# Router of a Flamingo block: ranks from bfloat16 marks added up on TensorE, scores from x itself, only selected rows normalized

## The chip, the cores and the metric

The kernel runs on one core of a Trainium2 chip. The metric is the device time in microseconds of one execution. The engines work side by side, each in its own order: TensorE (PE in the profile, its weight loads PEld), VectorE (DVE), ScalarE (ACT), GpSimd (POOL) and SyncE (SP), which issues most of the transfers.

## The reference, cut to what matters

`x` is 2 batches of 2048 rows of 512 floats. Four stages update it; the change lies between the first and the second.

```python
x = x + tanh(g_xattn[0]) * L0_xattn(layernorm(x), ctx)       # stage 1: cross attention, 16 heads
x = x + tanh(g_ffn[0])   * L0_ffn(layernorm(x), ...)         # stage 2: only 256 rows of a batch
x = x + tanh(g_xattn[1]) * L1_xattn(layernorm(x), ctx)       # stage 3
x = x + tanh(g_ffn[1])   * L1_ffn(layernorm(x), ...)         # stage 4

def L0_ffn(x, w_router, ...):           # x is already the layernorm of the stream
    scores = x @ w_router
    _, idx = top_k(scores, 256)         # in falling order; equal scores by index
    x_sel = x[idx]
    h = rmsnorm(x_sel, g1)              # then attention with a causal mask over the 256, and a gated FFN
    ...
    return x.at[idx].set(x_proc)        # all other rows come back as they are
```

So stage 2 needs, for each batch, the rank of every row's score among 2048, the 256 rows with the highest scores in order of rank, and for all rows `x + tanh(g)*layernorm(x)`.

## The kernel before, in words

The rows lie in 32 tiles of 128 rows (`x[0]` to `x[31]`, fp32, all in SBUF during stage 1), four tiles to a block of 512 rows, four blocks to a batch: eight blocks, n = 0 to 7, with `b, blk = divmod(n, 4)`.

`cross_attention` (L213) runs over units: 16 per block, one per head. In each unit it makes the scores on PE (`sc`, L271), the negated row maxima on DVE (`nmx`, L116), the exponentials on ACT (`A`, L119), their reciprocal sums on DVE (`rden`, L127), the scaling on POOL (`A`, L128), and two units later the transposes on PE (`tp`, L289) with their copy on DVE (`AT`, L290). Every fourth unit the values follow (`po`, L297, copied by ACT, L305), and after a block's sixteenth the output projection (`pp`, L315), which DVE adds to `x` (L324). The front of the next block (row statistics, `xn` by L101, transposes `ptr`, queries `pq` by L248) lies in between.

At the end of each unit `beside(u)` is called. It takes two steps of the generators in `pending`. After the last `x` of block n (L325) `router(n, tiles)` is put there. Its steps before the change:

- statistics of the block's four tiles of `x`, `rstd` (`rsqrt`, L82: one instruction on DVE, a power on POOL), and `keep_mul`, `keep_add` (L450 to L454);
- for each tile: the normalized rows `xn` (L101), stored to `xn_d` (L460); their dot product with `w_router` (`ws`, L462, its accumulator is the `score`); then ACT makes `x*keep_mul + keep_add` in place (L466), stored to `x_d` (L473), from which stage 3 reads;
- `spread` (L497): the block's 512 scores are laid along the free axis of all partitions: four transposes of a broadcast column (`pb`, L78) and a copy by ACT (`sb`, L504). `sb` holds the scores of the batch so far;
- `count` (L490): one DVE instruction compares a stretch of `sb` with a tile's own scores, one per partition, and sums over the stretch into a column of `cnt`. Every earlier tile is compared with the new 512 scores, and each new tile with all scores so far; for a tile with itself, `jd` (L514) does it twice, masked with `before` and `after`, so that equal scores go by index;
- after a batch's last block `add_up` sums `cnt` to `rank` (L520), and `gather` makes one-hot rows of the ranks (`oh`, L537), multiplies them with row numbers on PE (`pi`, L541), and fetches the 256 rows from `xn_d` into `xs` by two indirect transfers (L557).

PSUM during stage 1: `mm` has two buffers, `sc` four, and the tag `o` two, which `tp`, `po`, `pb` and `pi` share.

The order on each engine is fixed ahead of time by a planner. It goes by the order in the program, but takes a later instruction first where the earlier one is not ready by its reckoning: in the trace the statistics of the first two tiles of block 7 stand at 521.9 us, ahead of the `x` of its third tile at 527.9 us, though the program has them after.

After block 7 there is no further unit. `while pending: beside(None)` then runs the last router to its end. Stage 2 begins with loads of `wqkv` (L654) and with `rms_block(xs, ...)` (L626): squares on ACT (L631), `rsqrt`, `hn` on DVE (L634), transposes (`ptr`, L110) and `hT` (L639), from which PE makes the values `pv` (L674).

Of the kernel before, what the change touches and what calls it, by code (L numbers as in the profile page):

```python
# [10 lines left out]
F32 = mybir.dt.float32  # L11
# [32 lines left out]
def flamingo_kernel(ctx: ExitStack, tc: tile.TileContext, a: dict, out: bass.AP):  # L44
# [329 lines left out]
    score = selp.tile([P, NT], F32, name="score")  # L374
    xs = [selp.tile([P, D], F32, name=f"xs{i}") for i in range(4)]

    xn_d = [dramp.tile([S, D], F32, name=f"xn_d{b}") for b in range(B)]
    x_d = [dramp.tile([S, D], F32, name=f"x_d{b}") for b in range(B)]

    idx = selp.tile([P, 4], mybir.dt.uint32, name="idx")  # L380
# [11 lines left out]
    with ExitStack() as st:  # L392
# [11 lines left out]
            allow_small_or_imprecise_dtypes=True,  # L404
        )

        before = rp.tile([P, P], F32, name="before")
        nc.gpsimd.memset(before, 1.0)
        nc.gpsimd.affine_select(
            out=before,  # L410
            in_=before,
            compare_op=ALU.is_gt,
            fill=0.0,
            base=0,
            pattern=[[-1, P]],
            channel_multiplier=1,
        )
        after = rp.tile([P, P], F32, name="after")
        nc.gpsimd.memset(after, 1.0)
        nc.gpsimd.affine_select(  # L420
# [21 lines left out]
        def router(n, tiles):  # L442

            b, blk = divmod(n, NBLK)
            t0 = n * TB
            mv, rstd = ln_stats([x[t0 + i] for i in range(TB)], "ln2")

            keep_mul = rp.tile([P, TB], F32, name="keep_mul", tag="keep_mul", bufs=2)
            keep_add = rp.tile([P, TB], F32, name="keep_add", tag="keep_add", bufs=2)
            nc.vector.tensor_scalar(keep_mul, rstd, gf[0], None, ALU.mult)  # L450
            nc.vector.scalar_tensor_tensor(
                keep_add, mv[:, :, 0], -1.0, keep_mul, ALU.mult, ALU.mult
            )
            nc.vector.tensor_scalar(keep_mul, keep_mul, 1.0, None, ALU.add)  # L454
            yield
            for i in range(TB):
                t = t0 + i
                xn = act.tile([P, D], F32, name="xn2", tag="xn2", bufs=2)
                normalize(xn, x[t], mv, rstd, i)
                nc.sync.dma_start(out=xn_d[b][ts(t - b * TPB, P), :], in_=xn)  # L460
                ws = act.tile([P, D], F32, name="ws2", tag="ws2", bufs=1)
                nc.vector.scalar_tensor_tensor(  # L462
                    ws, xn, 1.0, w_router, ALU.mult, ALU.mult,
                    accum_out=score[:, t : t + 1],
                )
                nc.scalar.activation(  # L466
                    x[t],
                    x[t],
                    AF.Identity,
                    scale=keep_mul[:, i : i + 1],  # L470
                    bias=keep_add[:, i : i + 1],
                )
                nc.sync.dma_start(out=x_d[b][ts(t - b * TPB, P), :], in_=x[t])  # L473
                yield
            for work in ranks(b, blk):
                work()
                yield

# [1 line left out]

        def ranks(b, blk):

            done, end = blk * BLK, (blk + 1) * BLK

            def own(t):
                return score[:, b * TPB + t : b * TPB + t + 1]

            def count(t, lo, hi, op, k):  # L490
                junk = rp.tile([P, S], BF16, name="junk", tag="junk", bufs=2)
                nc.vector.tensor_scalar(
                    junk[:, lo:hi], sb[b][:, lo:hi], own(t), None, op, ALU.add,
                    accum_out=cnt[b][:, t, k : k + 1],
                )

            def spread():  # L497
                if blk == 0:
                    sb[b] = rp.tile([P, S], F32, name="sb", tag="sb")
                    cnt[b] = rp.tile([P, TPB, 7], F32, name="cnt", tag="cnt")  # L500
                    nc.gpsimd.memset(cnt[b], 0.0)
                pb = ps_o.tile([P, BLK], F32, name="pb", tag="o")
                bcast_rows(pb, score[:, ds(b * TPB + blk * TB, TB)], ident)
                nc.scalar.copy(sb[b][:, done:end], pb)  # L504

            def new(t):
                lo, hi = t * P, (t + 1) * P
                if lo > 0:
                    count(t, 0, lo, ALU.is_ge, 0)
                if hi < end:  # L510
                    count(t, hi, end, ALU.is_gt, 1)
                jd = rp.tile([P, 2, P], BF16, name="jd", tag="jd", bufs=2)
                for k, (op, m) in enumerate(((ALU.is_ge, before), (ALU.is_gt, after))):
                    nc.vector.scalar_tensor_tensor(  # L514
                        jd[:, k, :], sb[b][:, lo:hi], own(t), m, op, ALU.mult,
                        accum_out=cnt[b][:, t, 2 + k : 3 + k],
                    )

            def add_up():
                nc.vector.tensor_reduce(rank[:, ts(b, TPB)], cnt[b], AX.X, ALU.add)  # L520
                gather(b)

            work = [spread]
            work += [
                lambda t=t: count(t, done, end, ALU.is_gt, 3 + blk - t // TB)
                for t in range(blk * TB)
            ]
            work += [lambda t=t: new(t) for t in range(blk * TB, (blk + 1) * TB)]
            return work + [add_up] if blk == NBLK - 1 else work

        def gather(b):

# [2 lines left out]
            for t in range(TPB):  # L535
# [4 lines left out]
                for r in range(2):  # L540
                    nc.tensor.matmul(  # L541
                        pi[r],
                        oh[:, ts(r, P)],
                        place[:, t, :],
                        start=(t == 0),
                        stop=(t == TPB - 1),
                    )
            pl = rp.tile([P, 2, 2], F32, name="pl", tag="pl")
            for r in range(2):
                nc.vector.tensor_copy(pl[:, r, :], pi[r])  # L550
# [5 lines left out]
            for r in range(2):  # L556
                nc.gpsimd.indirect_dma_start(  # L557
                    out=xs[b * 2 + r],
                    out_offset=None,
                    in_=xn_d[b][:, :],  # L560
                    in_offset=bass.IndirectOffsetOnAxis(
                        ap=idx[:, b * 2 + r : b * 2 + r + 1], axis=0
                    ),
# [33 lines left out]
    with ExitStack() as st:  # L597
# [25 lines left out]
        def wide(name):  # L623
            return keepp.tile([P, DC, BLK], F32, name=name, tag="wide", bufs=2)

        def rms_block(tiles, gcol, dst, pool, ps, tag, name):  # L626

            ss = pool.tile([P, 4], F32, name=name + "_ss", tag="rms_ss")
            hn = [pool.tile([P, D], F32, name="hn", tag="hn", bufs=4) for _ in tiles]
            for i, t in enumerate(tiles):  # L630
                nc.scalar.activation(hn[i], t, AF.Square, accum_out=ss[:, i : i + 1])  # L631
            r = rsqrt(4, ss, 1.0 / D, 1e-6, small, name + "_r")
            for i, t in enumerate(tiles):
                nc.vector.tensor_scalar(hn[i], t, r[:, i : i + 1], None, ALU.mult)  # L634
            transpose_block(
                ps,
                tag,
# [6 lines left out]
        with ExitStack() as sa:  # L644
# [19 lines left out]
            for k in (0, 2):  # L664
                make_causal_mask(nc, mask[:, k, :], NEG)

            hT = wide("hT")
            rms_block(xs, g1, hT, act, ps_tp, "tp", "rms1")

            v2 = act.tile([P, 4, D], F32, name="v2")  # L670
            for i in range(4):
# [687 lines left out]
```

## Time and profile before

| What | Value |
|---|---|
| Median of 3 runs | 1853.16 us (1852.38 to 1861.52) |
| Profiled execution: time, span | 1854.16 us, 1852.5 us |
| Busy, of the span | PE 90%, DVE 71%, ACT 57%, POOL 28% |
| Stage 1 with all routers | 0 to about 565 us |
| Counting: instructions of L492, of L514 | 102, 64 |
| One-hots, products with row numbers | 32, 64 |
| Stage 2 after the gather | 573 to about 827 us |

The span is what the profiler records between the first and the last instruction; the execution's own time has 1.7 us around it. Busy time of an engine counts only where it computes; PE's records overlap, so that a busy PE is not a PE at its limit. In the timeline a row has its start, its length, the engine, the line of the program, output and inputs by name, shapes, and in brackets how long the engine stood idle before it and for whom.

### The profile page before, as it was taken

The page shows a single profiled execution, that of the slowest core. Times are in us where ns is not written, and L with a number is a line of the kernel's source. Part 1 is how long each engine was busy: PE and PEld are TensorE (multiplying, and loading weights), DVE is VectorE, ACT ScalarE, POOL GpSimd, SP SyncE. Part 2 cuts the span into 40 slices and gives each one's busy share as a digit, 9 for nine tenths or more (in the row PEclk, how much of TensorE's full clock was granted, in tenths as well). Part 3 has the DMA queues.
Part 4 walks back from the last instruction along what each step waited for, and adds up shares of the span by engine and source line. Part 5 has one row for each costly group of instructions (what it writes and reads, how often), then busy time and mean ns, then how long its engine had stood idle before and what let it go on. Part 6 is the DMA issues. An engine that isn't in the chain of part 4 may idle for free.

```text
span 1852.5 us, 24500 instructions
## 1 busy us (share of the span) xinstructions
PE 1660.6 (90%) x7706; PEld 832.8 (45%) x7706; DVE 1311.2 (71%) x2769; ACT 1050.8 (57%) x3065; POOL 527.4 (28%) x666
## 2 busy tenths in 40 slices
PE   6989988888836989989999999999999999898969
PEld 3544544444413444445544454444444454443423
DVE  5777897887783642224537779889888888876966
ACT  2745544354501535304537778878787787754556
POOL 4534434342300320032214333322423243220200
PEclk9999999899967889999999999999999999998989
DMA  7011011011144009330011233334133133155465
GB/s 287 1 46 47 1 47 46 12 46 47 46 139 156 1 9 314 112 91 23 26 35 55 97 114 105 128 120 154 52 135 127 77 109 123 74 203 205 150 229 191
DMA packets 98456, 184.36 MB, mean 100 GB/s; under 512 B 11327, under 2 KB 30527, under 8 KB 94614
## 3 DMA queue, kind: packets, MB, share of 16 engines
q1 hardware_dynamic: 97430, 180.70, 28.1%
q0 software_dynamic: 896, 2.10, 0.6%
q8 instruction: 61, 1.00, 0.2%
q14 instruction: 69, 0.57, 0.1%
HBM read 108.31 MB, written 74.45 MB: 99 GB/s over the span
## 4 chain that ended last, share of the span: by engine, by line
PE 34%; DVE 14%; DMA 6%; ACT 5%; issue 2%; POOL 2%; SPq 1%; POOLq 0%; DVEq 0%; ACTq 0%
PE pp L315 8%; PE pq L248 7%; DVE h L1018 3%; PE ph L1002 3%; PE sc L271 2%; PE po L297 2%; PE pu L875 2%; PE pw L875 2%; PE acc L861 2%; PE tp L289 2%; PE po L1231 1%; DMA hf<-h_d 1%; DMA x<-h_d 1%; DVE u L1012 1%; DMA hq<-hq_d 1%
## 5 line engine op out<-in xcount | busy, mean ns | idle before, releaser
L119 ACT ACTIVATE A<-sc,nmx 128x128 f32<-128x128 f32 x1024 | 362.9, 377 | 171.7 <-DVE nmx L116 149.8
L128 POOL TENSOR_TENSOR A<-A,rden 128x512 f32<-128x512 f32 x256 | 274.4, 1073 | 479.9 <-DVE rden L127 373.1
L315 PE MATMUL pp<-L_wo,OT 128*128 128x512 f32 x768 | 365.9, 610 | 12.7 <-DVE x L324 4.7
L248 PE MATMUL pq<-xnT,L_wq 128*128 128x512 f32 x768 | 358.0, 612 | 0.2 <-ACT xnT L237 0.2
L119 ACT ACTIVATION_READ_ACCUMULATOR A<-sc,nmx 128x1 f32 x1024 | 221.4, 216 | 0.0
L248 PEld LDWEIGHTS pq<-xnT,L_wq 128*128 128x128 f32 x768 | 145.7, 197 | 159.6 <-issue 151.7
L116 DVE TENSOR_REDUCE nmx<-sc 128x4 f32<-128x512 f32 x256 | 169.2, 678 | 66.6 <-PE sc L271 66.5
L290 DVE COPY AT<-tp 128x512 f32<-128x512 f32 x256 | 172.8, 677 | 55.5 <-PE tp L289 55.1
L315 PEld LDWEIGHTS pp<-L_wo,OT 128*128 128x128 f32 x768 | 139.0, 195 | 159.6 <-issue 134.9
L1018 DVE SCALAR_TENSOR_TENSOR h<-u,cw,h 128x512 f32<-128x512 f32 x256 | 191.4, 782 | 5.6 <-ACT h L1014 5.1
L289 PE MATMUL tp<-ident,A 128*128 128x128 f32 x1024 | 164.3, 282 | 28.7 <-POOL A L128 26.6
L271 PE MATMUL sc<-L_kT,qT 32*128 32x128 f32 (+1 forms) x2048 | 164.0, 291 | 8.1 <-ACT A L119 5.1
L271 PEld LDWEIGHTS sc<-L_kT,qT 32*128 32x128 f32 (+1 forms) x2048 | 130.8, 189 | 87.2 <-issue 59.3
L289 PEld LDWEIGHTS tp<-ident,A 128*128 128x128 f32 x1024 | 119.3, 143 | 103.9 <-issue 48.0
L1231 PE MATMUL po<-w2q,hq 128*128 128x512 bf16 x512 | 121.2, 392 | 18.2 <-DVE hq L1213 8.5
L1014 ACT ACTIVATE h<-u,cb,cw 128x512 f32<-128x512 f32 x128 | 99.2, 809 | 64.7 <-DVE u L1012 60.1
L1002 PE MATMUL ph<-xiT,w1q 128*128 128x512 bf16 x512 | 125.1, 381 | 2.6 <-DVE u L1012 2.3
L297 PE MATMUL po<-AT,L_v 128*32 128x512 f32 (+1 forms) x512 | 115.9, 623 | 7.9 <-DVE AT L290 7.5
L305 ACT COPY OT<-po 128x512 f32<-128x512 f32 x96 | 55.7, 588 | 101.4 <-PE po L297 100.9
L1012 DVE TENSOR_TENSOR u<-ph,inv_b 128x512 f32<-128x512 f32 x128 | 85.1, 683 | 31.8 <-PE ph L1002 26.9
L1011 POOL COPY u<-carry 128x2 f32<-128x2 f32 x128 | 49.2, 386 | 192.0 <-DVE h L1018 159.6
L311 POOL TENSOR_TENSOR x<-x,L_bo 128x512 f32<-128x512 f32 x64 | 87.3, 1382 | 33.8 <-DMA x<-x_d 14.3
(216 smaller groups left out, 2203.3 us busy)
## 6 DMA issues: line engine op xcount, KB each, us to landing
h_d<-h SPq DMA_DIRECT2D x28, 1024.0 KB, 3.9
x_d<-x SPq DMA_DIRECT2D x64, 256.0 KB, 2.5
hf<-h_d SPq DMA_DIRECT2D x64, 256.0 KB, 3.3
x<-x_d SPq DMA_DIRECT2D x61, 256.0 KB, 4.5
x<-h_d SPq DMA_DIRECT2D x48, 256.0 KB, 5.7
x<-in_x SPq DMA_DIRECT2D x32, 256.0 KB, 5.4
xn_d<-xn SPq DMA_DIRECT2D x32, 256.0 KB
xf<-x_d SPq DMA_DIRECT2D x32, 256.0 KB, 3.8
```

Source lines behind the costliest of these rows:

```text
L116: nc.vector.tensor_reduce(nmx, sc, AX.X, ALU.max, negate=True)
L119: nc.scalar.activation(out_tile[:, h, :], sc[:, h, :], AF.Exp, bias=nmx[:, h : h + 1], accum_out=den[:, h : h + 1],)
L128: nc.gpsimd.tensor_tensor(out_tile, out_tile, rden.unsqueeze(2).to_broadcast([P, n, width]), ALU.mult,)
L248: nc.tensor.matmul(pq, W.wq[:, d, ts(e, P)], xnT[:, d, :], start=(d == 0), stop=(d == DC - 1),)
L271: nc.tensor.matmul(sc[h][:, t, :], qT[e % cpg][r, ts(t, P)], W.kT[r, b, e, :], start=True, stop=True,)
L289: nc.tensor.transpose(tp[:, t, :], A[:, t, :], ident)
L290: nc.vector.tensor_copy(AT, tp.rearrange("p t n -> p (t n)"))
L297: nc.tensor.matmul(po[h * dh : (h + 1) * dh, :], W.v[:, b, ts(hd, dh)], AT[c * hpc + h], start=True, stop=True,)
L315: nc.tensor.matmul(pp, OT[e][:, ts(i, P)], W.wo[:, e, :], start=(e == 0), stop=(e == nE - 1),)
L1002: nc.tensor.matmul(ph, w1q[:, d, ts(c, P)], xiT[g][:, d, :], start=(d == 0), stop=(d == DC - 1),)
L1018: nc.vector.scalar_tensor_tensor(z, u[:, ds(k, BLK)], cw[:, c, k : k + 1], z, ALU.mult, ALU.add)
L1231: nc.tensor.matmul(po, rows(c), w2q[:, c, :], start=(c == 0), stop=(c == HC - 1))
```

## The change

- Each comparison writes its marks, 0 or 1 in bfloat16, and does not sum them. A product on PE with a column block of 32 ones (`onesb`) adds up the marks over the partitions, so that one PSUM row holds, for 512 rows of x, how many of the tile's 128 rows go before each. Earlier tiles against the new scores go to partitions `32*blk` on (`old`); new tiles against all scores so far go to partitions `32*c` for block c (`new`). The sums stay in `cnt` (128 x 512), and after the last block four products with `pick`, a matrix that selects partitions 0, 32, 64 and 96, turn them into `rank`. A tile with itself needs one masked comparison (`tie`) instead of two.
- `marks` has four buffers, `tie` four; `junk` and `jd` had two each.
- The score is worked out from `x`: `rstd*(x.w) - mean*rstd*sum(w)`. `x` itself is stored to `x1_d`, and the row for stage 3 goes to a tile of its own, `xo`.
- The gather fetches from `x1_d`; the 512 selected rows get their layer norm after it, and the mean square of the normalized row is taken from its variance, so that the squares on ACT fall away for this call of `rms_block`.
- There are more and smaller steps: two for each tile of the scores, one for two marks, and `gather` pauses after every fourth one-hot.

```diff
+        w_sum = rp.tile([P, 1], F32, name="w_sum")
+        nc.vector.tensor_reduce(w_sum, w_router, AX.X, ALU.add)
+        onesb = rp.tile([P, 32], BF16, name="onesb")
...
 # router
-            mv, rstd = ln_stats([x[t0 + i] for i in range(TB)], "ln2")
...
             for i in range(TB):
-                xn = act.tile([P, D], F32, name="xn2", tag="xn2", bufs=2)
-                normalize(xn, x[t], mv, rstd, i)
-                nc.sync.dma_start(out=xn_d[b][ts(t - b * TPB, P), :], in_=xn)
+                t = x[t0 + i]
+                nc.vector.bn_stats(st[:, i, :], t)
+                nc.vector.bn_aggr(mv[:, i, :], st[:, i, :])
+                yield
                 ws = act.tile([P, D], F32, name="ws2", tag="ws2", bufs=1)
                 nc.vector.scalar_tensor_tensor(
-                    ws, xn, 1.0, w_router, ALU.mult, ALU.mult,
-                    accum_out=score[:, t : t + 1],
+                    ws, t, 1.0, w_router, ALU.mult, ALU.mult, accum_out=dot[:, i : i + 1]
                 )
+                nc.sync.dma_start(
+                    out=x1_d[b][ts(t0 + i - b * TPB, P), :], in_=t
+                )
+                yield
+            rstd = rsqrt(TB, mv[:, :, 1], 1.0, 1e-5, small, "ln2_rstd")
...
+            nc.vector.scalar_tensor_tensor(shift, mv[:, :, 0], -1.0, rstd, ALU.mult, ALU.mult)
+            nc.vector.tensor_tensor(dot, dot, rstd, ALU.mult)
+            nc.vector.scalar_tensor_tensor(
+                score[:, ds(t0, TB)], shift, w_sum, dot, ALU.mult, ALU.add
+            )
...
+            for i in range(TB):
+                yield
+                xo = act.tile([P, D], F32, name="xo", tag="xo", bufs=2)
                 nc.scalar.activation(
-                    x[t],
-                    x[t],
+                    xo,
+                    x[t0 + i],
...
 # ranks
+            def goes_before(to, t, c0, c1, op):
+                nc.vector.tensor_scalar(to, sb[b][:, c0:c1], own(t), None, op)
+            def counted(psum, c, to, m, **kw):
+                nc.tensor.matmul(psum[32 * c : 32 * c + 32, to], onesb, m, **kw)
...
+            for j in range(blk):
+                m = marks()
+                for i in range(TB):
+                    goes_before(m[:, ts(i, BLK)], j * TB + i, lo, end, ALU.is_le)
+                    old.append(m[:, ts(i, BLK)])
+                    if i % 2:
+                        yield
...
+                po = ps_o.tile([P, BLK], F32, name="old", tag="o")
+                for i, m in enumerate(old):
+                    counted(po, blk, slice(0, BLK), m, start=(i == 0), stop=(i == len(old) - 1))
+                nc.vector.tensor_copy(cnt[b][rows, :], po[rows, :])
+                yield
...
+                goes_before(m[:, 0:mid], t, 0, mid, ALU.is_lt)
+                if mid < end:
+                    goes_before(m[:, mid:end], t, mid, end, ALU.is_le)
+                tie = rp.tile([P, P], BF16, name="tie", tag="tie", bufs=TB)
+                nc.vector.scalar_tensor_tensor(
+                    tie, sb[b][:, ts(t, P)], own(t), after, ALU.is_equal, ALU.mult
+                )
...
+            pn = ps_o.tile([P, BLK], F32, name="new", tag="o")
+            for i, m in enumerate(new):
+                for c in range(blk + 1):
+                    counted(pn, c, slice(0, BLK), m[:, ts(c, BLK)], start=(i == 0), ...)
+            for i, m in enumerate(ties):
+                counted(pn, blk, ts(i, P), m, start=False, stop=(i == TB - 1))
+                nc.vector.tensor_tensor(cnt[b][rows, :], pn[rows, :], cnt[b][rows, :], ALU.add)
...
+                pr = ps_o.tile([P, TB, NBLK], F32, name="pr", tag="o")
+                for q in range(TB):
+                    nc.tensor.matmul(
+                        pr[:, q, :], cnt[b][:, ts(q, P)], pick, start=True, stop=True
+                    )
...
 # gather
+                if t % 4 == 3:
+                    yield
-                    in_=xn_d[b][:, :],
+                    in_=x1_d[b][:, :],
...
 # start of stage 2
+            for b in range(B):
+                rows = xs[2 * b : 2 * b + 2]
+                mv, rstd = ln_stats(rows, f"lns{b}")
+                for i, t in enumerate(rows):
+                    normalize(t, t, mv, rstd, i)
+                ms = row.tile([P, 2], F32, name="ms", tag="ms")
+                nc.vector.tensor_tensor(ms, mv[:, :, 1], rstd, ALU.mult)
+                nc.vector.tensor_tensor(ms, ms, rstd, ALU.mult)
+                rs = rsqrt(2, ms, 1.0, 1e-6, row, "rms1_r")
...
-            rms_block(xs, g1, hT, act, ps_tp, "tp", "rms1")
+            rms_block(xs, g1, hT, act, ps_tp, "tp", "rms1", r)
```

## The prediction

> **What bounds the kernel now.** I read the page first, then the busy time of each engine in stretches that follow the router, the groups of VectorE (DVE), the waits, and the timeline of the end of stage 1. The page's chain of waits reaches back only to 686 us, so stage 1 is read from stretches. One stretch runs from a router's first store of `xn` to the next router's; columns are length, then busy us and count of PE, PEld, DVE, ACT, POOL, then TensorE clock, DMA share, GB/s.
>
> ```profile
> 116.90:174.10 57.20, 51.70 (x308) 27.42 (x308) 46.77 (x123) 30.88 (x141) 24.87 (x23) 1.00 0.10 38
> 174.10:235.60 61.50, 55.62 (x308) 29.84 (x308) 50.09 (x133) 31.18 (x141) 24.93 (x23) 0.94 0.10 35
> 235.60:300.70 65.10, 56.11 (x308) 29.76 (x308) 55.32 (x141) 31.16 (x141) 24.99 (x23) 0.95 0.09 33
> 300.70:378.90 78.20, 67.60 (x340) 37.52 (x340) 66.58 (x170) 31.62 (x141) 27.37 (x26) 0.87 0.10 34
> ```
>
> The attention of a block is the same in all four; only the counting grows. The period grows with DVE, so counting is paid for, though PE is busy 90% of each row. The end of stage 1, on the timeline (start, us, engine):
>
> ```profile
> 532.81 0.18 DVE L97 BATCH_NORM_AGGREGATE ln_mv<-ln_st 128x2 f32<-128x6 f32 x1
> ...
> 540.73 0.75 DVE L492 TENSOR_SCALAR_CACHE_REDUCE junk<-sb,score 128x512 bf16<-128x512 f32 x1 [1.19 <-ACT sb L504]
> ...
> 548.73 1.81 DVE L492 TENSOR_SCALAR_CACHE_REDUCE junk<-sb,score 128x1536 bf16<-128x1536 f32 x1
> ...
> 559.96 0.27 DVE L520 TENSOR_REDUCE rank<-cnt 128x16 f32<-128x112 f32 x1
> 560.27 4.29 DVE L537 TENSOR_SCALAR oh<-iota_r,rank 128x256 bf16<-128x256 f32 x16
> ...
> 565.74 1.04 POOL L557 DMA_INDIRECT xs<-xn_d,idx  x1 [31.46 <-DVE idx L555]
> ...
> 573.44 0.63 ACT L631 ACTIVATE hn<-xs 128x512 f32<-128x512 f32 x1 [0.52 <-DMA xs<-xn_d,idx]
> ...
> 575.52 1.67 DVE L634 TENSOR_SCALAR hn<-xs,rms_r 128x512 f32<-128x512 f32 x4 [1.16 <-POOL rms_r L87]
> ...
> 580.40 14.47 PE L674 MATMUL pv<-wqkv,hT 128*128 128x512 f32 x32
> ```
>
> Here nothing covers the router: DVE alone sets the time from 532 to 565 us. Rows that price the new operations:
>
> ```profile
> L1107 DVE TENSOR_SCALAR hi<-hf x32: 388/416/1462, 1080.3 to 1585.3; 128x512 bf16<-128x512 f32 x32
> L841 DVE TENSOR_SCALAR w1q<-wq x8: 683/685/694, 724.3 to 732.2; 128x1024 bf16<-128x1024 f32 x8
> L514 DVE SCALAR_TENSOR_TENSOR jd<-sb,score,after 128x128 bf16<-128x128 f32 x32 | 14.3, 447 | 0.0
> L297 PE MATMUL po<-AT,L_v 128*32 128x512 f32 x256 | 35.1, 605 | 2.5 <-DVE AT L290 2.4
> PE pb L78 <- DVE ws L462: 21.2, 13, 2.5
> ```
>
> **What the Trainium skill says.** "VectorE: DVE Perf Modes", on the perf-mode tier table, gives `tensor_scalar` on fp32 in SBUF two elements a cycle. The trace agrees for fp32 read and bf16 written: 388 to 685 ns from 512 to 1024 columns, 0.58 ns a column. The counting instruction that also sums goes from 0.67 us (512) to 1.73 us (1536), start to start: 1.04 ns a column. "TensorE: Matmul & The Clock Gate", Part 3, says that products which write to different groups of 32 PSUM partitions run at the same time, and gives 2.38 times for three. The trace agrees: `po`, which does so, has 605 ns a record but 35.1 us for 256, 0.14 us each, against 0.43 us start to start for `pp` over all columns. Part 1 of that page says that an idle window halves the array's clock; the rows of the tail show a granted clock of 0.50.
>
> **The change, part by part.** I price by start-to-start distances, since durations overlap: old count 0.13 us + 1.04 ns a column; mark 0.12 us + 0.58 ns a column (0.42 for 512: four `hn`, which like a mark take one scalar per partition, in 1.67 us); `jd` 0.27 us; copy from PSUM 0.68 us.
>
> *Counting on DVE.* Before, block blk has 4·blk counts of 512, four tiles' counts of own and earlier columns (1536, 3584, 5632, 7680 columns in 6 or 7 instructions each) and eight `jd`: 4.6, 9.5, 14.3, 19.2 us for blk 0 to 3; the timeline gives 540.73 to 559.9 = 19.2. After: 4·blk marks of 512 (0, 1.7, 3.3, 5.0), a copy of their sums from blk 1 on (0.7), marks over 4·512·(blk+1) columns in 7 instructions (2.0, 3.2, 4.4, 5.6), four `tie` (1.1), one add (0.7), and in blk 3 0.2 for ranks: 3.8, 7.4, 10.2, 13.3 us. Saved 0.8, 2.1, 4.1, 5.9.
>
> *Scores from x.* Four normalizations of `xn2` go (0.45 each); two more instructions on 128x4 come (0.3): 1.5 us a block. `ws`, the two stores a tile and ACT's four `Identity` stay in number; SP's queue carries the same bytes. DVE saves 2.3, 3.6, 5.6, 7.4 us a block.
>
> *Worth under the attention (routers 0 to 5).* The first three rows grow by 4.3 and 3.6 us for 4.9 and 4.8 us of counting: 0.8 us a DVE us. Six routers save 2.3+3.6+5.6+7.4+2.3+3.6 = 24.8, worth 20 us (bounds 12 and 25: part may be PE's already).
>
> *Products on PE.* A bf16 product of 512 columns takes 0.216 us (eight `ph` in 1.73 us on the chain). For `old` they fall into one column group, 0.9, 1.7, 2.6 us; for `new` blk+1 groups go together, 0.9 us, or 0.9·(blk+1) if not; ties 0.25; the four fp32 products with `pick` about 1.0. Per block 1.1, 2.0, 2.8, 4.7 us; routers 0 to 5: 13.7 us, 19.7 if serial. PE has some 6 us free per stretch and works in order; I charge 0.7 of it, 9.6 us (bounds 0 and 19.7).
>
> *New waits.* Each block has two sums in PSUM of tag "o" (one in blk 0), which `tp`, `po` and `pb` share over two buffers. While one is filled and copied, transposes have one buffer left. PE, in order, waits for DVE's marks before each sum; `tp`, the next scores and queries stand behind, and through `nmx` ACT and POOL. The trace shows such a wait only for `pb` behind `ws`: 21.2 us in 13 waits, 3 us a block, up to 2.5 each. `pb` now waits once for all four columns, so a little of that goes. Per wait from -0.5 to 2.5 us; I take 0.5, twice in six blocks: 6 us. Net for routers 0 to 5: 20 - 9.6 - 6 = 4.4 us.
>
> *Router 6.* From 504 to 521 us DVE is full with its counts, and PE stands 5.57 us behind `x` (L324) at 521 us, then runs at half clock for some 5 us. 5.6 DVE us saved end that sooner: 5 us (2 to 8).
>
> *Router 7, uncovered.* The last tile's `x` is ready at 532.05 us. Now: stats 0.9, `rsqrt` 1.3 (the last `ws` beside POOL's power), three small ones 0.5, four `pb` 1.0, copy 0.6: first mark at 536.5 instead of 540.73, 4.2 us earlier. Marks, ties and copy 12.4; then PE's last products 1.0, the add 0.7, `pick` 1.3, ranks and hops 0.5: 16.0 against 19.5 to the first `oh`, 3.5 us. PE at half clock needs 0.43 us a product, 5.2 for the twelve old ones, the pace of the marks, so it trails. Together 7.7 us (5 to 10). One-hots and gather are as before; the new yields change nothing where there is no attention. Weights `wqkv` start when `idx` is made (565.6), land after 10.9 us and move with it. In between, `L_wo` (2 MB) may still be moving; `hT` leaves 3 us of cover today.
>
> *Rows normalized after the gather.* Batch 0 lands at 365 us and is hidden. Batch 1, after its second landing: stats 0.9, eps and power 1.3, two normalizations 0.9, two small and eps 0.5, power 1.1, `hn` 0.8: 5.5, against 3.8 today (573.4 to 577.2, ACT's squares gone): 1.8 us lost (0 to 3). Stages after that see the same work.
>
> Sum: 4.4 + 5 + 7.7 - 1.8 = 15.3 us. The profiled run took 1854.2 us (span 1852.5), 1.0 over the median 1853.2; 1854.2 - 15.3 = **1839 us**. A measurement of this kernel tells about 0.5%, 9.3 us, from no change.
>
> **Rivals.**
> 1. *PE and PSUM eat the covered gain.* The 90% busy rows speak for it. Products at full weight (13.7) and 1 us a wait (12) leave 20 - 25.7 = -6, router 6 is worth 3: -6 + 3 + 7.7 - 1.8 = 3 faster, 1851. Chance 0.22.
> 2. *Slower: PE waits in order for marks* with a buffer of "o" held, in every covered block. At 2.5 us a wait, 12 waits cost 30; with serial products (19.7) the covered part is 20 - 49.7 = -30, router 6 gains nothing: -30 + 5.9 = 24 slower, 1878. It decides from about (20 - 9.6 + 10.9)/12 = 1.8 us a wait. The `pb` row speaks for it; against it, marks end sooner than counts and PE has queries to do. Chance 0.13.
> 3. *The broken lump gains more.* The fourth row is 13.1 us longer than the third for 4.9 us of counting: 16 `oh` in step with 32 `pi`, clock 0.87. Yields after every fourth `oh` let `nmx` through; but `pi` holds both buffers of "o" until its end, so `tp` still waits. If it goes, 9 more: 1830. Chance 0.12.
> 4. *The marks get no double rate.* Then 512 cost 0.58 and the gain is the accumulator's 0.08 a count: counting saves little, 1848 at best. Sixteen `oh` in 4.29 us, 0.27 for 256 columns with such a scalar, speak against it. Chance 0.03.
>
> The forecast keeps 0.50. The range, 1822 to 1861, takes rival 3 with the good ends of router 6 and 7 below, rival 1 and a wait of 2 us above; it leaves out the worst of rival 2. Over 0.5% faster: most of the forecast (0.48), rival 3 (0.12): 0.61 with a little of rival 1. Slower: rival 2 and a bad end of rival 1, 0.14. The rest, 0.25, within.
>
> **What would show it.** Marks of 512 near 0.42 us apart; stretches of about 56, 60, 63, 76 us; first mark of router 7 some 4.5 us after its `x`; from there to `oh` 16 us; second landing to `pv` 9 us. PE records of `new` beginning almost together show the packing. Wrong is the forecast if PE's waits for marks pass 20 us in all, if `tp` waits on "o" longer than now, or if `pv` waits for `wqkv`.

## Result and the profile after

The changed kernel takes **1834.55 us** in the median of 6 runs (1832.29 to 1836.62), against 1853.66 for the kernel before in the same session: a ratio of 0.989, interval 0.987 to 0.991, or 17 to 24 us saved. Foretold were 1839, 1822 to 1861. The profiled execution took 1832.29 us, its span is 1830.2.

The stretches now run from the last `x` (L324) of a block to that of the next; columns as in the prediction (length, then busy us and count of PE, PEld, DVE, ACT, POOL, then TensorE clock, DMA share, GB/s). First the stretch beside router 3 and the one beside router 6, before:

```profile
296.45:374.70 78.25, 67.61 (x342) 37.52 (x341) 66.62 (x168) 31.62 (x141) 27.41 (x25) 0.87 0.10 34
...
490.71:531.30 40.59, 28.43 (x120) 12.37 (x118) 32.91 (x90) 11.06 (x40) 5.30 (x5) 0.87 0.14 52
```

and blocks 0 to 3 and router 6 after:

```profile
113.62:172.80 59.18, 54.34 (x318) 29.20 (x317) 44.26 (x103) 30.73 (x141) 24.10 (x22) 0.91 0.10 37
172.80:232.97 60.17, 54.02 (x326) 28.38 (x325) 46.42 (x109) 30.62 (x141) 24.38 (x22) 0.94 0.10 36
232.97:297.58 64.61, 57.52 (x334) 30.44 (x333) 51.39 (x113) 30.90 (x141) 24.33 (x22) 0.89 0.09 34
297.58:363.22 65.64, 56.96 (x366) 29.19 (x364) 56.93 (x127) 29.13 (x133) 24.63 (x21) 0.92 0.09 33
...
478.79:512.36 33.57, 29.37 (x144) 11.93 (x142) 24.62 (x58) 10.86 (x40) 5.17 (x5) 0.95 0.17 63
```

Rows 1 to 3 have 2.5, 3.6 and 3.9 us less of DVE, and are 1.9 us longer, 1.3 and 0.5 shorter. The fourth is 12.6 us shorter, and router 6's 7.0. Nearly all of the gain lies in these two. The prediction had named router 6; for routers 0 to 5 together it had 4.4 us.

The end of stage 1 after, on the timeline (start, us, engine):

```profile
512.36 0.75 DVE L324 SCALAR_TENSOR_TENSOR x<-pp,gate,x 128x512 f32<-128x512 f32 x1
...
515.66 0.66 DVE L96 BATCH_NORM_STATS2 lns_st<-xs 128x6 f32<-128x512 f32 x1
516.23 0.15 DVE L85 TENSOR_SCALAR ln_rstd_e<-ln_mv 128x4 f32<-128x4 f32 x1
...
518.06 1.12 PE L78 MATMUL pb<-ident,score 128*128 128x128 f32 x4 [5.74 <-DVE score L476]
...
519.66 0.56 ACT L524 COPY sb<-pb 128x512 f32<-128x512 f32 x1
520.25 5.83 DVE L511 TENSOR_SCALAR marks<-sb,score 128x512 bf16<-128x512 f32 x13
520.79 5.00 PE L517 MATMUL old<-marks,onesb 128*32 128x512 bf16 x12 [1.62 <-DVE marks L511]
...
535.89 4.29 DVE L597 TENSOR_SCALAR oh<-iota_r,rank 128x256 bf16<-128x256 f32 x16
...
558.05 2.17 PE L751 MATMUL pv<-wqkv,hT 128*128 128x512 f32 x3
```

The last `x` ends at 513.1; the first mark begins 7.1 us later, and 15.6 us after that the first one-hot. The row of 13 marks has twelve of 512 columns and one of 1664, which begins at 525.0: the twelve are 4.75 / 12 = 0.40 us apart, and PE's twelve `old` keep their pace. From the last `x` to `pv` it takes 45.7 us, 49.1 before. From `pv` to the end of the span both kernels take 1272.1 us.

The groups of the new operations over the whole profile (count, then busy us and mean ns, then idle before them), and one line of the waits:

```profile
L511 DVE TENSOR_SCALAR marks<-sb,score 128x512 bf16<-128x512 f32 x50 | 27.7, 610 | 1.5 <-ACT sb L524 1.4
L517 PE MATMUL old<-marks,onesb 128*32 128x512 bf16 x48 | 14.1, 436 | 3.6 <-DVE AT L290 2.0 <-DVE marks L511 1.6
L517 PE MATMUL new<-marks,onesb 128*32 128x512 bf16 x80 | 10.9, 411 | 5.1 <-DVE marks L511 4.4 <-DVE AT L290 0.6
PE pb L78 <- DVE score L476: 5.7, 1, 5.7
```

PE waited 1.6 and 4.4 us for marks, in all blocks together. `new` goes in groups: 411 ns a record, but 0.14 us each.

### The profile page after: what moved, and what is told of

Read it like the earlier page. It is cut to its first block, busy times and chain, and to the rows that moved or that the text cites. A ratio compares the mean times of both kernels' runs of the same rounds, so it can differ in the third digit from the quotient of the medians.

```text
span 1830.2 us, 24658 instructions
## 1 busy us (share of the span) xinstructions
PE 1663.7 (91%) x7836; PEld 832.5 (45%) x7882; DVE 1278.9 (70%) x2591; ACT 1046.0 (57%) x3057; POOL 524.2 (29%) x668
## 4 chain that ended last, share of the span: by engine, by line
PE 36%; DVE 12%; DMA 6%; ACT 5%; issue 2%; POOL 2%; SPq 1%; POOLq 0%; DVEq 0%; ACTq 0%
PE pp L315 8%; PE pq L248 8%; PE ph L1079 3%; DVE h L1095 3%; PE po L297 2%; PE sc L271 2%; PE pu L952 2%; PE acc L938 2%; PE pw L952 2%; PE tp L289 2%; PE po L1308 2%; DMA x<-h_d 1%; DMA h_d<-h 1%; DMA hf<-h_d 1%; DMA hq<-hq_d 1%
## 5 line engine op out<-in xcount | busy, mean ns | idle before, releaser
L128 POOL TENSOR_TENSOR A<-A,rden 128x512 f32<-128x512 f32 x256 | 274.6, 1075 | 471.5 <-DVE rden L127 361.6
L248 PE MATMUL pq<-xnT,L_wq 128*128 128x512 f32 x768 | 346.7, 600 | 0.2 <-ACT xnT L237 0.2
L119 ACT ACTIVATION_READ_ACCUMULATOR A<-sc,nmx 128x1 f32 x1024 | 225.9, 221 | 0.0
L271 PEld LDWEIGHTS sc<-L_kT,qT 32*128 32x128 f32 (+1 forms) x2048 | 117.8, 197 | 89.7 <-issue 69.1
L271 PE MATMUL sc<-L_kT,qT 32*128 32x128 f32 (+1 forms) x2048 | 147.7, 301 | 10.0 <-DVE qT L256 7.7
L297 PE MATMUL po<-AT,L_v 128*32 128x512 f32 (+1 forms) x512 | 121.2, 671 | 9.8 <-DVE AT L290 8.1
```

Source lines behind the costliest of these rows:

```text
L119: nc.scalar.activation(out_tile[:, h, :], sc[:, h, :], AF.Exp, bias=nmx[:, h : h + 1], accum_out=den[:, h : h + 1],)
L128: nc.gpsimd.tensor_tensor(out_tile, out_tile, rden.unsqueeze(2).to_broadcast([P, n, width]), ALU.mult,)
L248: nc.tensor.matmul(pq, W.wq[:, d, ts(e, P)], xnT[:, d, :], start=(d == 0), stop=(d == DC - 1),)
L271: nc.tensor.matmul(sc[h][:, t, :], qT[e % cpg][r, ts(t, P)], W.kT[r, b, e, :], start=True, stop=True,)
L297: nc.tensor.matmul(po[h * dh : (h + 1) * dh, :], W.v[:, b, ts(hd, dh)], AT[c * hpc + h], start=True, stop=True,)
```

## The experiments

All times are medians, ratios are against the kernel before on the same chip, with a 95% interval. Stretches and chains come from one profile each.

### Was it the pauses between one-hots? (theory A: yes; theory B: the shorter counting)

`e1_no_pauses` takes the pauses out of the changed kernel, `e2_before_pauses` puts them into the kernel before.

```diff
 # e1                                   # e2 has these two lines added, and gather() as steps of its own
-                if t % 4 == 3:
-                    yield
```

> The changed kernel, but gather makes its sixteen one-hots without a pause, as before. Theory A, the pauses gave the 12 us that stretches 3 and 4 (last x of block 2 to last x of block 4) lost: 10 to 12 us slower than the changed kernel's 1834.6, about 1845, those two stretches together near 137 us instead of 126. Theory B, the shorter counting gave them: 1835 within 3 us, the two stretches near 127.

> The kernel before, with nothing changed but a pause in gather after every fourth one-hot. Theory A (pauses): 10 to 12 us faster than before, about 1842, the stretches 3 and 4 together near 127 us instead of 138. Theory B (shorter counting): 1853 within 3 us.

Measured: e1 1831.89 us (0.9853, 0.983 to 0.988), e2 1855.83 (0.9991, 0.997 to 1.001); router 3's stretch is 68.3 in e1 and 77.9 in e2, against 65.6 in the changed kernel and 78.2 before. The pauses are neither needed nor enough: theory A fell. At most they bring 2.7 of the 12.6 us. (The two stretches that the expectations add up are 143.3 us before and 130.3 after, not 138 and 126.) Theory B isn't shown by this, since e1 keeps everything else that changed.

### What do products and the marks' rate weigh?

`e3_products_twice` makes every product with ones twice (`pick` holds 0.5), `e4_marks_summed` has each mark also sum its stretch: in its tail the marks of 512 columns are 0.67 us apart, as the counts before were, and not 0.40. Theory C: PE sets the time, so that products cost more than their records; theory D: they mostly hide.

```diff
 # e3
-                nc.tensor.matmul(psum[32 * c : 32 * c + 32, to], onesb, m, **kw)
+                for k in range(2):
+                    nc.tensor.matmul(psum[32 * c : 32 * c + 32, to], onesb, m, ...)
 # e4
-                nc.vector.tensor_scalar(to, sb[b][:, c0:c1], own(t), None, op)
+                one = rp.tile([P, 1], F32, name="one", tag="one", bufs=8)
+                nc.vector.tensor_scalar(
+                    to, sb[b][:, c0:c1], own(t), None, op, ALU.add, accum_out=one
+                )
```

> The changed kernel with every product of marks with ones issued twice and pick filled with 0.5, so that ranks are the same; DVE and ACT do what they did. Theory C, the products on PE cost under the attention what they take: their busy time of 14 (old) + 11 (new) + 3 us is doubled, 18 to 22 of it in routers 0 to 5 and some 5 in router 7 at half clock: 18 to 28 us slower than 1834.6. Theory D, PE's free time takes them: only router 7 shows it, 3 to 6 us slower.

> The changed kernel with each mark instruction also summing over its columns into a cell that nothing reads[...]; products, pauses and waits as in the changed kernel. DVE gets about 0.25 us more for 512 columns: 2, 4, 6 and 8 us in blocks 0 to 3. Theory E, a DVE us under the attention is worth 0.8 us: routers 0 to 5 cost 18 to 20 us more, router 6 5 and router 7 7: about 30 slower. Theory F, it is worth next to nothing there since PE bounds the covered blocks: only routers 6 and 7 show it, 8 to 12 us slower.

Measured: e3 1849.0 us (0.9938, 0.992 to 0.996), 14 more than the changed kernel by medians of two sessions, 9 by the ratios, between C and D; in its profile `pv` is 13.5 us later, 2.3 of that in the tail and 0.4 beside router 6, so that routers 0 to 5 lose about 11. Not all of it need be the products': the planner put DVE's instructions in another order in five of the seven stretches, and 6.5 of the 11 lie in router 3's. e4 1854.71 (0.9981, 0.996 to 1.000), 20 more by medians, 17 by the ratios, between E and F; every engine keeps the changed kernel's order in all seven stretches. In its profile `pv` is 25 us later: 6.5 in router 3's stretch, 6.4 in router 6's, 7.6 in the tail, and from 0 to 2.2 in each of the others. DVE's time costs most in those three places. But what is lost to the products (11) and what the faster marks bring under the attention (11) cancel, and the 12.8 us gained in routers 0 to 5 have no source. The next runs looked for it.

### The two halves of the change

`e5_scores_alone` is the kernel before with the score part (and its eight more steps a router), `e6_marks_alone` the changed kernel without that part and those steps. Theory G: the unexplained part comes with the scores; theory H: with the counting on PE.

```diff
 # e5, in the kernel before             # e6 has this taken back in the changed kernel
-            mv, rstd = ln_stats([x[t0 + i] for i in range(TB)], "ln2")
+            for i in range(TB):
+                nc.vector.bn_stats(st[:, i, :], t)
...
+                yield
+                nc.vector.scalar_tensor_tensor(ws, t, 1.0, w_router, ..., accum_out=dot[:, i : i + 1])
...
+                yield
```

> The kernel before with the score part alone: scores from x, x itself stored and gathered, selected rows normalized after the gather, the router's smaller steps up to its scores; counting, ranks and one-hots as before. With the twice issued products and the summed marks accounted for, about 13 us of the routers 0 to 5 are unexplained. Theory G: they come from the score part, because pb then waits once for all four columns and DVE has 1.5 us less a block: pv starts 10 to 13 us earlier than before, time about 1841 to 1844, and PE's waits for ws go from 21 us to below 8. Theory H: they come with the counting on PE (one masked comparison instead of two, copies gone to fewer, PE free of nothing else): then this kernel is worth what the prediction put for it, 1.5 us a block and 1 us at the tail less 1.8 for the rows: 1849 to 1853.

> The changed kernel with the score part taken back: rows normalized before the scores, xn stored and gathered, squares of the selected rows as before; marks, products, ranks and pauses as changed. Theory G: routers 0 to 5 gain nothing, since the faster marks (11) pay for the products (11): what is left is router 6 (7) and the tail (about 4): 1842 to 1846. Theory H: routers 0 to 5 keep 10 or more of their 12.8: 1834 to 1838.

Measured: e5 1849.02 (0.996, 0.995 to 0.997), e6 1843.31 (0.9937, 0.992 to 0.996). By its time e5 fits theory H, and e6 fits theory G, so that neither holds for both: each half gains, 6.7 and 12.4 us. PE's waits of `pb`, which G blamed, are down from 21.2 us to 0.3 under the attention of e5 and bring no more than this. The profiles said where to look. Router 3's stretch is 69.3 us in e5, though its counts are as slow as before; and its one-hots come later, from 352.7 us on, among the next block's work. e5 has more steps.

### The steps alone

`e8_steps_in_before` puts eight more steps into each router of the kernel before, two behind the statistics of each tile, and changes no computation. `e9_coarse_steps` takes these steps out of the changed kernel. Theory P: the place of the work; theory S: the saved work.

```diff
 # e8
-            mv, rstd = ln_stats([x[t0 + i] for i in range(TB)], "ln2")
+            for i in range(TB):
+                nc.vector.bn_stats(st[:, i, :], x[t0 + i])
+                nc.vector.bn_aggr(mv[:, i, :], st[:, i, :])
+                yield
+                yield
+            rstd = rsqrt(TB, mv[:, :, 1], 1.0, 1e-5, small, "ln2_rstd")
 # e9, in the changed kernel: twice in the loop over a block's tiles
-                yield
```

> The kernel before with eight more steps in each router and nothing else: after a tile's statistics it yields twice, as the changed kernel does for statistics and dot product. The score part alone moved the last x of block 7 by 11 us, of which 9 in the stretch of router 3 and 9 in that of router 6, and 4 lost in that of router 4. Theory P (place of the work): this came because eight more steps put counting and gather four units later, into the front of the next block: rank of batch 0 at about 352 instead of 344 us, router 3's stretch at about 70 instead of 78, router 6's below 36, time about 1846 to 1850. Theory S (saved work): it came with the four normalizations and pb's waits: then stretches as before within 2 us, 1853 to 1857.

> The changed kernel with the two yields of each tile's scores taken out: statistics and dot products of a block come in one step, as before the change. Theory P: rank of batch 0 falls back to about 340 us, ahead of the block's end, router 3's stretch grows from 65.6 to about 72, router 6's to 38: time 1840 to 1845. Theory S: nothing but a burst of 5 us on DVE behind each block's x: 1834 to 1838.

Measured: e8 **1834.09** us (0.9874, 0.986 to 0.989), e9 1838.51 (0.9889, 0.987 to 0.991). Eight more steps give the kernel before the whole gain, with all its sums on DVE, more than theory P asked. But without them the change keeps most or all of its own, with router 3's stretch at the 73.1 us that P foretold and a time next to theory S's: the two gains do not add up. Router 3's and router 6's stretches of e8:

```profile
295.43:361.72 66.29, 52.26 (x322) 26.64 (x320) 62.77 (x157) 30.68 (x141) 25.34 (x23) 0.92 0.09 32
...
476.29:510.26 33.97, 24.45 (x120) 10.84 (x118) 31.23 (x84) 10.86 (x40) 5.82 (x5) 0.95 0.17 63
```

DVE is busy 63 and 31 us, as much as before but for 4 and 2, and yet they are 12.0 and 6.6 us shorter. Over the stretches of routers 0 to 5 DVE is busy 308.2 us before and 308.0 in e8, which takes 14.3 us less. The granted clock is not the reason: router 3's stretch had 0.869 before and 0.875 in e1, and e1 is 9.9 us shorter there. The reason for router 6 is in the order on DVE. PE's output projections of block 7 before, and then in e8 (the brackets: idle before, and for whom):

```profile
514.68 1.98 PE L315 MATMUL pp<-L_wo,OT 128*128 128x512 f32 x4 [0.68 <-ACT OT L305]
521.40 9.86 PE L315 MATMUL pp<-L_wo,OT 128*128 128x512 f32 x16 [4.74 <-DVE x L324]
```

```profile
495.31 1.98 PE L315 MATMUL pp<-L_wo,OT 128*128 128x512 f32 x4 [0.73 <-ACT OT L305]
498.83 3.70 PE L315 MATMUL pp<-L_wo,OT 128*128 128x512 f32 x8 [1.54 <-DVE x L324]
504.72 3.70 PE L315 MATMUL pp<-L_wo,OT 128*128 128x512 f32 x8 [2.18 <-DVE x L324]
```

Before, DVE made all counts of router 6 first, and the first `x` of block 7 at 520.6. `pp` has two buffers, so that PE stood 4.74 us for that `x` and then made sixteen `pp` at 0.62 us each instead of 0.46, at a granted clock of 0.72 (521.4 to 531.3 us) against 1.00 in e8. In e8 two `x` go between the counts, at 498.0 and 503.9 us. The changed kernel has it so too (one at 499.7, two at 507.8 and 509.1), and PE waits 0.43 us.

Router 3's lump held other work: the row maxima and reciprocals of the attention. Before:

```profile
346.13 0.74 DVE L324 SCALAR_TENSOR_TENSOR x<-pp,gate,x 128x512 f32<-128x512 f32 x1
346.79 1.54 DVE L537 TENSOR_SCALAR oh<-iota_r,rank 128x256 bf16<-128x256 f32 x5
...
353.92 0.35 DVE L537 TENSOR_SCALAR oh<-iota_r,rank 128x256 bf16<-128x256 f32 x1 [0.51 <-PE pi L541]
354.28 1.26 DVE L116 TENSOR_REDUCE nmx<-sc 128x4 f32<-128x512 f32 x2
354.53 1.04 POOL L128 TENSOR_TENSOR A<-A,rden 128x512 f32<-128x512 f32 x1 [8.48 <-DVE rden L127]
355.06 0.37 ACT L119 ACTIVATE A<-sc,nmx 128x128 f32<-128x128 f32 x1 [8.86 <-DVE nmx L116]
...
362.33 0.75 DVE L324 SCALAR_TENSOR_TENSOR x<-pp,gate,x 128x512 f32<-128x512 f32 x1
```

and in e8:

```profile
352.89 0.71 DVE L324 SCALAR_TENSOR_TENSOR x<-pp,gate,x 128x512 f32<-128x512 f32 x1
359.57 0.88 DVE L544 TENSOR_SCALAR oh<-iota_r,rank 128x256 bf16<-128x256 f32 x3 [0.92 <-PE pi L548]
360.64 0.88 DVE L544 TENSOR_SCALAR oh<-iota_r,rank 128x256 bf16<-128x256 f32 x3 [0.18 <-PE pi L548]
361.72 0.75 DVE L324 SCALAR_TENSOR_TENSOR x<-pp,gate,x 128x512 f32<-128x512 f32 x1 [0.20 <-PE pi L548]
```

Before, thirteen of the sixteen one-hots and their products go between the second and the third `x` of block 4, one by one in step with scores. The row maxima stand behind them on DVE, ACT waits 8.86 us for these and POOL 8.48, and 16.2 us lie between the two `x`. PE waited for no `x` there. In e8 most of them come around the fourth, the last, beside queries and projections; the distance of third and fourth is 8.8 us.

### Each place by itself

`e11_steps_router_3` and `e12_steps_router_6` have the eight steps in one router only.

```diff
 # e8 -> e11 (n == 3), e12 (n == 6)
+                if n == 3:
                     yield
                     yield
```

> The kernel before with the eight more steps in router 3 alone, the one that ends in the one-hots of batch 0. In the kernel before, the 16 one-hots go in one row between the second and the third x of block 4 (346 and 362 us), each in step with a product pi and two half-speed scores. Theory P, place by place: router 3's stretch falls from 78 to 66 to 70, router 6's stays at 40 with PE's wait of 4.7 us for x: time 1843 to 1848. Theory W (the whole order from router 3 on shifts): router 6's stretch falls too, without steps of its own: 1834 to 1838. Rival: the gain of the steps comes from all routers, so that here nothing is seen: 1853 to 1857.

> The kernel before with the eight more steps in router 6 alone, which runs beside the attention of block 7. In the kernel before, DVE makes all counts of router 6 (503.8 to 520.6 us) ahead of the first x of block 7; PE stands 4.74 us for that x and then makes sixteen pp in 9.9 us at half clock. Theory P: with the steps the first x goes between the counts, PE's wait is gone, the stretch from the last x of block 6 to that of block 7 falls from 40.6 to 34, the tail grows by up to 1.5: 5 to 7 us saved, time 1848 to 1851. Rival: as with router 3 alone, most of it is given back in the tail, since counts then remain after the last x: 1853 to 1857.

Measured: e12 1846.36 us (0.995, 0.993 to 0.997), 8.3 saved. Its stretch is 33.9 us, as foretold, with the full counts of before, and the tail grew by 1.3. The time is below the range foretold: in the profile routers 0 to 2, whose order is as before, took 3.7 us more and the part behind `pv` 6.0 less, so that the stretch is the firmer figure. PE's rows:

```profile
517.52 3.70 PE L315 MATMUL pp<-L_wo,OT 128*128 128x512 f32 x8 [1.54 <-DVE x L324]
523.41 5.40 PE L315 MATMUL pp<-L_wo,OT 128*128 128x512 f32 x8 [2.18 <-DVE x L324]
```

So router 6's 7 us are shown to be a matter of order. e11 1853.36 (0.9988, 0.998 to 1.000), a miss, in the rival's range: router 3's stretch falls to 66.4 us, 11.8 less, but the stretches of routers 4 and 5, whose code is as before, grow by 3.0 and 5.9, and 2.3 us of gain are left. Router 4's has the rest of router 3's one-hots and its gather. Router 5's has the same instructions in the same order on every engine; here it is before, and then in e11:

```profile
434.23:490.71 56.48, 49.89 (x294) 26.46 (x293) 45.38 (x119) 28.96 (x137) 17.78 (x17) 1.00 0.10 38
```

```profile
425.29:487.70 62.41, 57.20 (x294) 30.68 (x293) 45.82 (x119) 29.07 (x137) 17.74 (x17) 0.86 0.09 35
```

What differs is the granted clock, 0.86 against 1.00, and with it PE's busy time; why it was lower is not shown. With the steps in all routers (e8) the two stretches take 114.6 us, 1.4 less than before. Whether moved one-hots need steps in the routers behind them is open.

### Scores from x, with the steps held equal

`e10_marks_and_steps` is e6 with the eight steps of e8: against the changed kernel, it lacks only the score part.

```diff
 # e6 -> e10: the diff of e8, in e6
```

> The changed kernel with the scores taken from normalized rows again (xn normalized, stored and gathered, squares as before), but with eight steps more for the statistics, so that it has as many steps as the changed kernel: against the marks alone it has only the steps more, against the changed kernel only the scores less. Theory P: under the attention the place of the work counts and the score part is worth nothing: router 3's stretch 65 to 68, last x of block 7 at 509 to 513 us, time 1829 to 1835, 8 to 14 below the marks alone. Theory A (both parts add, steps included in the scores): marks alone less nothing: 1840 to 1845.

Measured: **1828.62** us (0.9852, 0.982 to 0.989), last `x` of block 7 at 510.9, `pv` at 556.4. Time and router 3's stretch (64.2) lie just below what theory P foretold. It is 5.9 us below the changed kernel by medians, with intervals that overlap: the score part gained nothing there, though in routers 0 to 5 it takes 16.1 us of DVE's busy time away (303.2 to 287.0; these stretches got 2.9 us longer, at a lower granted clock, 0.925 against 0.967). Against e8, which has the steps but not the marks, the last `x` comes at 510.9 instead of 510.3 and the tail is 5.0 us shorter: with the steps equal, marks and products gain in the tail alone. With sums on DVE it even loses, e5 against e8 (0.996 against 0.987): 15 us. In the profiles that loss lies beside routers 1 and 3 to 5, 3 us each, while DVE is less busy and PE's clock lower (0.939 to 0.947 in all thirteen runs of e5, 0.951 to 0.956 in e8's four). Its cause was not found.

### Batch 0's rows normalized early

`e7_rows_early` is e1 with batch 0's selected rows treated in router 4 (behind its ranks, not in its first step as the expectation says).

```diff
+            if n == NBLK:
+                selected_rows(0)       # statistics, norms, mean square of batch 0's rows
+                yield
```

> The changed kernel without the pauses in the one-hots, and the statistics and norms of batch 0's selected rows put into router 4's first step instead of stage 2. In the changed kernel two of these statistics (0.66 us each, lns_st) stand in DVE's queue between the last scores of router 7 and its rsqrt. Theory E: they are the most of what the first mark of router 7 came late: it comes 1.2 us sooner after the last x, and about 1 us more is saved behind the second landing: 1830 to 1832.5, 2 us below the changed kernel. Rival: the first mark is held by the stores and POOL's power anyway, first mark moves by less than 0.4 us, time as the kernel without pauses (1832) or above, since router 4 is longer by 3 us.

Measured: **1827.86** us (0.9856, 0.983 to 0.988), the lowest median. The first mark comes 6.7 us after the last `x`, 0.45 sooner than in the changed kernel, where theory E wanted 1.2 and the rival less than 0.4. By medians e7 is 4 us below e1, but against the kernel before on their own chips the two are level (0.9856 and 0.9853), so that this gain is not shown.

## Why the prediction was right, and where it was not

The total was right, 1834.55 against 1839. The mechanism under the attention was not, and that the total came so near is in part luck: the sum had 8.4 us too little for routers 0 to 5 and 2.0 for router 6, 2.5 too much for the tail, and the profiled runs differ by 3.2 us more than the medians. Profiles side by side, in us (stretches by the router that runs in them; "coarse" is e9):

| | before | after | e8 steps | e9 coarse | e10 |
|---|---|---|---|---|---|
| routers 0 to 2 | 183.8 | 184.0 | 182.9 | 181.5 | 180.9 |
| router 3 | 78.2 | 65.6 | 66.3 | 73.1 | 64.2 |
| routers 4, 5 | 116.0 | 115.6 | 114.6 | 112.9 | 117.2 |
| router 6 | 40.6 | 33.6 | 34.0 | 34.7 | 34.0 |
| last `x` to `pv` | 49.1 | 45.7 | 50.5 | 44.8 | 45.5 |

- **The step that failed: "worth under the attention", 0.8 us for each of 24.8 DVE us.** It was read from how three rows grew, and taken as one price of DVE's time. After products and waits it left 2.1 us of gain for routers 0 to 2, 1.6 for router 3 and 0.5 for routers 4 and 5; -0.2, 12.6 and 0.4 came. So the miss is router 3, and e8 shows what is enough for it: with as much DVE time as before, in another place, routers 0 to 5 take 14.3 us less. Nor do they get shorter with less of it, the changed kernel against e10. But the price is not nothing: in e4, with the order held, 8.3 us more of DVE's busy time in routers 0 to 5 cost 11, more than half of it in router 3. DVE's time had its highest price where a lump of it stood ahead of what other engines waited for.
- **The rows that the price was read from grew in part with the clock.** Router 0's row had a granted clock of 1.00, the next two 0.94 and 0.95. e12 has the same instructions in the same order on every engine there, at 0.94:

```profile
113.22:172.87 59.65, 54.23 (x310) 28.45 (x309) 46.91 (x121) 31.04 (x141) 24.92 (x22) 0.94 0.10 36
```

It is 2.4 us longer (2.7 in e2), so that more than half of the first growth, 4.3 us, is not DVE's. The same order of routers 0 to 2 took 183.8, 183.8, 185.0 and 187.5 us in four profiles (before, e11, e2, e12), at 0.963, 0.963, 0.954 and 0.927: differences of this size in single stretches say little.
- **The term costed at nothing: the eight more steps.** The prediction named the yields of the one-hots alone, and only for router 7. The steps of the scores put counts and one-hots elsewhere in the order, and e8 shows that in the kernel before this is worth all the change is, 23.5 us. The change without them (e9) gains 19 as well: router 6 is cured there by shorter counts (34.7), router 3 only to 73.1. So how much of the 19 us the steps caused is no number: either alone would have brought about as much.
- **Products on PE**: 9.6 charged, about 11 by e3, in another order and with 6.5 in router 3 where 3.3 was charged; the size fits, and the runs don't show it more closely. `new` went in groups as the `po` row had said, 0.14 us each, in agreement with "TensorE: Matmul & The Clock Gate", Part 3, of the Trainium skill.
- **New waits**, 6 us charged for routers 0 to 5. There PE stood 2.6 us for `AT` ahead of sums, and with `tp` and `po` 1.7 us for `cnt`, the copy of a sum: 4.3 us in all, none of these waits over 1.1, where rival 2 needed 1.8 each. Waits for marks are 6.0 us, 5.4 of them in the tail (1.62 for the first `old`, 0.35 to 0.95 for `new`) and the rest beside router 6. The waits of `pb`, 21.2 us before, of which the prediction let a little go, are gone under the attention.
- **Router 6**: 5 foretold, 7.0 came. The wait for `x` behind DVE's counts was the right place (PE's own wait was 4.74 us; the prediction's 5.57 is the weight load's); but the counts need not be shorter (e12).
- **Router 7's first mark** was the mis-sized term: 4.2 us sooner foretold, 1.5 came. Statistics were put at 0.9 us from the last `x` to `rsqrt`; they took 3.1, since the statistics and dot product of the third tile too, and part of one `lns_st` of batch 0, stood behind that `x` on DVE. Laying out the scores took 2.2 instead of 1.6. e7 moves `lns_st`, and the 3.1 becomes 2.7.
- **Marks to one-hots**: 16.0 foretold, 15.6 measured. The marks of the tail take 0.42 us for 384 columns and 1.28 for 2048, 0.52 ns a column, which agrees with the two elements a cycle of "VectorE: DVE Perf Modes", perf-mode tier table, of the Trainium skill. Summing as well they take 1.04 ns a column (e4: 0.61 us for 384, 1.94 for 1664), and e4 pays 17 to 20 us for it. Rival 4 is out. This part is sure, since nothing covers it: e8, with all sums on DVE, has a tail of 50.5.
- **Rows normalized after the gather**: 1.8 us lost foretold, 2.0 measured (15.0 to 17.0 from `idx` to `pv`), of which 1.3 behind the second landing; the other 0.7 is the gather's own. `pv` did not wait for `wqkv`.
- **Rival 3**, the broken lump, came: 12.6 us in router 3's stretch, where it had put 9 more. What it named was in the way, the row maxima behind the one-hots; but what let them through was not the pauses (e1, e2).

Terms against what the profiles show: routers 0 to 5 4.4 against 12.8, router 6 5 against 7.0, tail 5.9 against 3.4, and 0.9 lost at the start of block 0: 15.3 against 22.3 in the profiles, 19.1 in the medians.

## What to carry to other kernels

Where engines work in a fixed order, ask of a covered helper not only how long it is but what stands behind it in the queue: here sixteen one-hots ahead of the row maxima, and router 6's counts ahead of an addition that PE waited for, cost about as much as all of the new arithmetic brought. Before replacing the arithmetic, try more steps that put it elsewhere; it is a cheap experiment and separates place from work. And a yield in a diff is a change of the schedule: give it a term in the sum.

## What the runs showed that was not expected

- Over the whole profile a mark of 512 columns has 610 ns a record in the mean of 50; the twelve in the tail have 478. The slow ones wait for POOL. Ten of the fifty, of 0.99 to 1.26 us, begin while POOL scales a tile `A` (L128), and each ends 0.28 us after that does. The other forty take 0.45 to 0.49 us, beside the attention or not; none begins while POOL is at work. The counts before, which also summed, took 0.71 to 0.75 us in all fifty cases, though 15 of them begin while POOL is at work. Four marks after, the first of them beside a scaling that ran from 317.53 to 318.57 us, and then three without one:

```profile
317.59 2.44 DVE L511 TENSOR_SCALAR marks<-sb,score 128x512 bf16<-128x512 f32 x4 [0.23 <-ACT sb L524]
...
326.03 1.26 DVE L511 TENSOR_SCALAR marks<-sb,score 128x512 bf16<-128x512 f32 x3
```

So in this kernel the faster instruction is the one that POOL holds up, and a rate read in a stretch without POOL does not carry over. It also bears on e4: its summing marks are not held (0.71 to 0.75 us), so that it gave DVE only 8.3 us more in routers 0 to 5 where 26 had been expected.
- Runs of one kernel follow their mean granted TensorE clock: e10's four took 1825.6, 1827.9, 1829.4 and 1836.5 us at 0.961, 0.958, 0.958 and 0.951. The part from `pv` to the end, whose work no experiment changes, took from 1266 (e12) to 1276 us (e9) in single profiles. So a single profile tells places, and medians tell totals.
